# A sequence model on one core: another order of work where the local attention stage begins, and seven tiles in which a second queue issues part of the ring transfers

## The chip, the cores and the metric

The kernel runs on one core of a Trainium2 chip. The metric is the device time of one execution in microseconds (us). Before the change it is 1805.12 us, the median of three runs (1803.43 to 1805.38).

## What is computed

Four sequences of 1024 positions and 256 features go through two blocks. The first is causal attention with 16 heads of width 16. The second has two layers; each is a local attention with 8 heads of width 64 in windows of 128 positions, and a gated feed-forward part.

```python
def _layer(x, wqkv, qs, ksc, wo, lg, lb, w1, b1, w2, b2):
    h = shift_token(x)
    q, k, v = jnp.split(h @ wqkv, 3, axis=-1)
    q = l2norm(q) * qs
    k = l2norm(k) * ksc
    q, k = rotary_xpos(q, k)
    o = local_attention(q, k, v)      # own window and the one before it
    x = x + o @ wo
    h = layernorm(shift_token(x)) * lg + lb
    a, g = jnp.split(h @ w1 + b1, 2, axis=-1)
    return x + (a * gelu(g)) @ w2 + b2

x = x + attn(layernorm(x))
x = x + ffn(layernorm(x))             # two times _layer
```

All data is 32-bit floating point.

## The kernel before

**Stages.** The causal attention runs first, in 16 chunks (4 sequences by 4 groups of heads). Then comes the local stage: 64 tiles of 128 positions (2 layers, 4 sequences, 8 windows), taken in groups of four that alternate between two sequences. The feed-forward work of a finished group is spread over later tiles by a table of places (`F_PLAN`, and `F_FIRST` for the first group), which `feed(n, place)` reads.

**Queues.** The order of instructions on each engine is that of the program text: each engine works through its own queue in order, and an instruction that waits holds up all that stands behind it on its engine. TensorE (PE) does the matrix products, VectorE (DVE) and ScalarE (ACT) the work on what PE leaves in PSUM, GpSimd (POOL) powers, rotations and scalings in SBUF, and SyncE (SP) issues nearly all transfers.

**One tile of the local stage.** In iteration n of the loop at L1408 the core makes q, k and v of tile n (`qkv_mm`, L234; `qkv_take`: squares on ACT, L249, three products for each of q and k on DVE, L251 and L257, a copy of v on ACT, L265) and rotates them (`rotate`: a reduction on DVE, L273, and four operations on POOL, the power L279 and the product L281 among them). Scores of tile n - 2 are made (`scores`, L397 or L412), softened (`soften`: DVE L428, ACT L435) and scaled (`scale_e`, L449, on POOL or DVE). The weights of tile n - 4 meet v (`weigh`, L482 or L508), ACT copies the products out (`loT`, L490 or L515), and `attend` multiplies them by the output weights (`pw`, L524).

**The ring.** Before q, k and the softened weights can be operands, they have to be transposed into `ring`, a buffer of three slots. From tile 7 on `stage(n, e)` does it: DVE transposes blocks of 32 by 32 into `turned` (L308, L322, L323, or L331 for a tile without earlier keys), and 16 transfers (L339, from SP) carry the blocks to their partitions. Each waits until DVE has filled `turned`; DVE does not refill it until the transfers have read it. Scores and products of the next iterations wait until they have landed.

**The first tiles.** For the first tiles, and the last ones, PE does the transposing, since there is no time for transfers yet: `turn(n)` for q and k of tiles 0 to 6, with one copy of q on ACT and one of k on DVE (L353 and L354; both on ACT for tile 0), and `turn_e` for the weights of tiles 0 to 3 (L461, copies L466, DVE for even c and ACT for odd c). These tiles also run with shorter distances: scores of tile n - 1 and products of tile n - 2 for tiles 0 to 3. In iterations below 7 all scores of a tile come first (`scores(w, 0)`, `scores(w, 1)`), then the products with v, then the softening.

**The handover.** The end of the causal stage overlaps with the first tiles of the local stage: tile 1's q, k, v are made (L1356) while DVE transposes the last result (`put_oT`, L1155), whose transfers to `oT` are issued by SP and ACT (L1159). After `out_b` (L809, L1179) the rest of the plan runs (L1362): the normalising of a pair of rows (`out_c`, L706), statistics of another pair (`out_s`: L698, L699, a power on POOL, L163) and the normalising of that pair. Two more pairs have their statistics and normalising in iterations 2 to 4 of the local loop (L1469 to L1474), at the end of an iteration.

**PSUM.** All products of the local stage take turns in eight banks (`one`). A product into a bank waits until its former content has been read.

Of the kernel before, what the change touches and what calls it, by code (L numbers as in the profile page):

```python
# [17 lines left out]
B, T, D = 4, 1024, 256  # L18
NW = T // P
# [22 lines left out]
GRP = 4  # L42

SEGQ, SEGK, NSEG = 2 * LH, 2 * LH + 4, 2 * LH + 8
FAST_QK = 7
FAST = (4, 2)
EARLY = 2
# [4 lines left out]
def kernel_body(  # L52
# [17 lines left out]
    nc = tc.nc  # L70
# [7 lines left out]
    x_keep = keep.tile([B, P, NW, D], F32, name="x_keep")  # L78
# [93 lines left out]
    N = len(wins)  # L172
# [128 lines left out]
            state[n, "blocks"] = [(1 - behind, own), (int(behind), state[b, "kv"])]  # L301
        state[b, "kv"] = own

    def stage(n, e):

        k0, k1 = NSEG, 0
        if n is not None:
            nc.vector.transpose(  # L308
                turned[:, SEGQ:NSEG].rearrange("p k j r -> p (k j r)"),
                state.pop((n, "rot")).rearrange("p a d -> p (a d)"),  # L310
            )
            settle(n)
            k0, k1 = SEGQ, NSEG
        if e is not None:
            for g in range(2):
                dst = turned[:, LH * g : LH * g + LH]
                src = state.pop((e, "e", g))
                if slim(e):


                    dst = dst.rearrange("p (h b) j r -> p h (b j r)", b=2)
                    nc.vector.transpose(dst[:, :, 0:NK], src[:, :, 0:NK])  # L322
                    nc.vector.transpose(dst[:, :, NK : 2 * P], src[:, :, 0:HALF_W])  # L323
                    continue
                if wins[e][3] == 0:
                    dst = dst.rearrange("p (h b) j r -> p h b (j r)", b=2)[:, :, 1, :]
                    src = src[:, :, P : 2 * P]
                else:
                    dst = dst.rearrange("p k j r -> p (k j r)")
                    src = src.rearrange("p h k -> p (h k)")  # L330
                nc.vector.transpose(dst, src)  # L331
            k0, k1 = 0, max(k1, SEGQ)
        if k1 == 0:
            return
        i = (n + 1 if n is not None else e) % 3
        for d in range(4):
            for a in range(4):
                j = (a + d) % 4
                nc.sync.dma_start(  # L339
                    ring[32 * j : 32 * j + 32, i, k0:k1, 32 * a : 32 * a + 32],  # L340
                    turned[32 * a : 32 * a + 32, k0:k1, j, :],
                )

    def turn(n):

        rot = state.pop((n, "rot"))
        for a, k in ((0, SEGQ), (1, SEGK)):
            pt = one(f"pt{a}_{n}")
            for i in range(4):
                nc.tensor.transpose(  # L350
                    pt[:, i * P : (i + 1) * P], rot[:, a, i * P : (i + 1) * P], ident
                )
            copy = nc.vector.tensor_copy if a and n else nc.scalar.copy  # L353
            copy(ring[:, (n + 1) % 3, k : k + 4], pt.rearrange("p (c n) -> p c n", c=4))  # L354
        settle(n)

# [312 lines left out]
    def f_start(G):  # L669

        sooner = 6 if G == 0 else 3 if G == len(groups) - 1 else 0
        return 3 * (GRP * G + GRP + 3) + 2 - sooner
# [18 lines left out]
    stats, last_x = {}, []  # L691
# [19 lines left out]
    with actx:  # L711
# [73 lines left out]
        NCH = B * NC4  # L785
# [500 lines left out]
        n = -1  # L1286
# [26 lines left out]
        with tc.manual_schedule(  # L1313
            engines={
                mybir.EngineType.PE, mybir.EngineType.Activation, mybir.EngineType.DVE,
                mybir.EngineType.Pool, mybir.EngineType.SP,
            }
        ):

            warm = one("warm")  # L1320
            for _ in range(WARM):
                nc.tensor.matmul(warm[:, 0:P], lhsT=ident, rhs=ident, start=True, stop=True)
            nc.gpsimd.memset(qbuf[0], 0.0)
            nc.gpsimd.memset(kbuf[0], -1.0)
            nc.gpsimd.memset(nmax, 0.0)
            clear()
            norm(0, 0, NW // 2)
            for t2 in range(2):
                prep_x(0, t2)
                prep_a(0, t2)  # L1330
            for i in range(4):
                project(0, 0, i % 2, i // 2)
            spread(0, 0, nc.scalar)
            norm(0, NW // 2, NW)
            for t2 in range(2, 4):
                prep_x(0, t2)
                prep_a(0, t2)
            for i in range(4):
                project(0, 0, i % 2, 2 + i // 2)
            for n in range(-1, NCH):  # L1340
                if n == NCH - 1:
                    inner.close()
                    g1, g2, g3, g4, g5 = (
                        ctx.enter_context(tc.tile_pool(name=f"g{i}", bufs=i, side="right"))
                        for i in range(1, 6)
                    )
                for u in range(NU):
                    pair(n, u, 0)
                    pair(n, u, 1)
                    m, w = (n, u - 1) if u else (n - 1, NU - 1)  # L1350
                    if m >= 0:
                        products(m, w)
                    for fn, a in plan[n][u]:
                        fn(*a)
            products(NCH - 1, NU - 1)
            qkv_mm(1)  # L1356
            put_out(NCH - 1, 1)
            put_oT(NCH - 1, 1)
            qkv_take(1)
            rotate(1)  # L1360
            for t2 in (2, 3):
                out_b(B - 1, t2)  # L1362
            for fn, a in [x for u in plan[NCH] for x in u]:
                fn(*a)

# [25 lines left out]
    with tc.manual_schedule(  # L1393
# [12 lines left out]
            return [w for w in range(N) if w + (soon if fast(w) else late) == n]  # L1406

        for n in range(f_start(len(groups) - 1) // 3 + F_END // 3 + 2):  # L1408
            if EARLY <= n < N:
                qkv_mm(n, range(n == EARLY, 3))  # L1410
                qkv_take(n)
                if n == half - 1:
                    load_attn(1)
            r, m = (
                w if 0 <= w < N and not own(w) else None
                for w, own in ((n - 1, fast_qk), (n - 3, fast))
            )
            first = feed(n, 0, True)
            if first:
                feed(n, 0)  # L1420
            stage(r, m)
            if 0 < n <= N and fast_qk(n - 1):
                turn(n - 1)
                if n == EARLY - 1:
                    qkv_mm(EARLY, range(1))
            late = FAST_QK <= n < N - 1
            if EARLY <= n < N and not late:
                rotate(n)
            for w in at(n, 10 * N, 2):
                for c in range(4):  # L1430
                    turn_e(w, c)
            if EARLY <= n < N - 1:
                transposed(n + 1)
            if n in (half - 8, half):
                load_tab(1, n // half)
            if not first:
                feed(n, 0)
            now, then = at(n, 2, 1), at(n, 4, 2)

            end = n >= N - 1  # L1440
            now.sort(key=lambda w: not (end and fast(w)))
            begin = n < FAST_QK
            for step in (1, 0) if begin else (0, 1):
                for w in now if step else ():
                    for g in range(2):
                        scores(w, g)
                        if not begin:
                            soften(w, g)
                for w in () if step else then:
                    for c in range(4):  # L1450
                        weigh(w, c)
            for w in now:
                for g in range(2) if begin else ():
                    soften(w, g)
                keep_edge(w)
            if late:
                rotate(n)
            for w in then:
                attend(w)
                if w == half - 1:  # L1460
                    load_out(1)
            if n in (half - 7, half + 1):
                scale_tab(1, n // half)
            if not end:
                feed(n, 1)
            for w in now:
                scale_e(w, 0)
                scale_e(w, 1, nc.vector if begin or end and fast(w) else nc.gpsimd)
            for t2, first in ((2, EARLY), (3, EARLY + 1)):  # L1469
                src = last_x[0][:, 2 * t2 - GRP : 2 * t2 - GRP + 2, :] if last_x else None  # L1470
                if n == first:
                    out_stats(B - 1, t2, src, f2)
                if n == first + 1:
                    out_norm(B - 1, t2, src)  # L1474
            if n == EARLY + 2:
                nc.sync.dma_start(x_keep[B - 1][:, GRP:NW], last_x.pop())
            if end:
                feed(n, 1)
            feed(n, 2)
# [72 lines left out]
```

## Time and profile before

| | us |
|---|---|
| median of the runs | 1805.12 |
| the profiled execution, whole | 1806.02 |
| its span, first to last instruction | 1803.9 |
| TensorE busy | 1766.8 (98%) |
| VectorE busy | 1331.1 (74%) |
| ScalarE busy | 1019.5 (57%) |
| GpSimd busy | 1106.9 (61%) |
| ring transfers: issues of 96 KB and of 64 KB | 880 and 48 |

The busy shares are averages over stages. The causal stage takes about the first 600 us, the local stage the rest. A window line below gives, for a stretch of time, the busy time and number of instructions of each engine in it, the clock that was granted to TensorE as a share of full speed, the busy share of the core's 16 DMA engines, and GB/s. A waits line gives an engine and line, what it waited for, the sum in us, how many times, and the longest. A timeline line gives start, duration, engine, line, operation, what it writes and reads, and in brackets the idle time of the engine before it with what ended it. ACTq and SPq are the queues of ACT and SP at work on issuing a transfer.

### The profile page before, as it was taken

To read this page: it belongs to the slowest core of one execution; us is meant where nothing else is said; L and a number is where in the kernel's file an instruction comes from. 1 tells how busy PE (TensorE), PEld (TensorE's weight loads), DVE (VectorE), ACT (ScalarE), POOL (GpSimd) and SP (SyncE) were. 2 spreads that over 40 slices of the span, in tenths; PEclk is the share of its full clock that TensorE was granted. 3 is DMA by queue.
4 is the path that set the end of the run, shared out by engine and by line. 5 is a ranking of instruction groups with operands and counts; after the bars stand their busy time and mean duration, and the time that the engine had idled before them with its cause. 6 is when DMAs were issued, how large, how long until landed. Compare 5 with 4: busy or idle time off the path is not lost.

```text
span 1803.9 us, 45874 instructions
## 1 busy us (share of the span) xinstructions
PE 1766.8 (98%) x16922; PEld 1044.7 (58%) x16922; DVE 1331.1 (74%) x4107; ACT 1019.5 (57%) x2557; POOL 1106.9 (61%) x1310
## 2 busy tenths in 40 slices
PE   9999999999999898999999999999999999999999
PEld 5444454555444464565665656666656656566566
DVE  6987987887786677686776877767767768678642
ACT  1677767777777454545546455555555454545621
POOL 3354586476476566665766766757667667577511
PEclk8999999999999999999999999999999999999999
DMA  4435344335222202555556556655666555656420
GB/s 118 129 93 172 97 102 129 118 93 154 81 78 73 80 1 46 90 99 90 93 90 102 101 103 120 112 102 96 134 118 115 109 100 112 116 96 119 94 49 24
DMA packets 811294, 178.04 MB, mean 99 GB/s; under 512 B 761568, under 2 KB 786128, under 8 KB 810688
## 3 DMA queue, kind: packets, MB, share of 16 engines
q1 hardware_dynamic: 810752, 174.79, 45.6%
q8 instruction: 135, 2.21, 0.5%
q14 instruction: 87, 0.71, 0.1%
q10 hardware_dynamic: 320, 0.33, 0.1%
HBM read 50.32 MB, written 29.29 MB: 44 GB/s over the span
## 4 chain that ended last, share of the span: by engine, by line
PE 85%; DVE 7%; SPq 2%; DMA 2%; ACT 1%; issue 1%; POOL 1%; ACTq 0%; DVEq 0%; POOLq 0%
PE pag L614 16%; PE pf L638 9%; PE t L994 8%; PE av L1055 7%; PE pw L524 6%; PE s L994 6%; PE pq L234 5%; PE pv L234 5%; PE pk L234 5%; PE plo L482 5%; PE ls L397 4%; PE pp L809 3%; SPq L339 2%; PE pv L809 2%; DVE s L1004 1%
## 5 line engine op out<-in xcount | busy, mean ns | idle before, releaser
L1015 ACT ACTIVATE et<-t 128x512 f32<-128x512 f32 x558 | 292.2, 601 | 78.2 <-PE s L994 58.7
L614 PE MATMUL pag<-hnT,w 128*128 128x512 f32 x704 | 312.2, 593 | 0.8 <-DVE hnT L598 0.8
L994 PE MATMUL t<-qbuf,kbuf 32*128 32x512 f32 (+1 forms) x1488 | 297.9, 503 | 0.6 <-DMA qbuf<-way 0.3
L994 PE MATMUL s<-kbuf,qbuf 16*128 16x512 f32 (+3 forms) x1440 | 295.4, 506 | 1.5 <-DMA qbuf<-img 1.5
L435 ACT ACTIVATE e<-e,lnmx 128x192 f32<-128x192 f32 (+2 forms) x512 | 224.1, 439 | 50.2 <-DVE lnmx L428 49.7
L614 PEld LDWEIGHTS pag<-hnT,w 128*128 128x128 f32 x704 | 131.4, 190 | 142.5 <-issue 133.0
L449 POOL TENSOR_SCALAR e<-e,lrsum 128x192 f32<-128x192 f32 (+2 forms) x484 | 195.3, 426 | 18.1 <-DVE lrsum L446 12.6
L994 PEld LDWEIGHTS t<-qbuf,kbuf 32*128 32x128 f32 x1488 | 147.4, 184 | 92.0 <-ACT et L1015 40.4
L279 POOL TENSOR_TENSOR rn<-ss,mhalf 128x16 f32<-128x16 f32 x64 | 188.2, 2940 | 5.3
L1074 POOL TENSOR_TENSOR avs<-avs,part 128x512 f32<-128x512 f32 (+2 forms) x105 | 117.7, 1121 | 114.2 <-ACT part L1073 113.7
L276 POOL TENSOR_TENSOR rot<-rot,m 128x1024 f32<-128x1024 f32 x64 | 151.5, 2367 | 55.0 <-DVE m L257 45.4
L638 PE MATMUL pf<-w,act 128*128 128x256 f32 x768 | 173.1, 379 | 0.0
L994 PEld LDWEIGHTS s<-kbuf,qbuf 16*128 16x128 f32 x1440 | 144.9, 184 | 33.1 <-DVE nmax L1004 6.0
L638 PEld LDWEIGHTS pf<-w,act 128*128 128x128 f32 x768 | 145.8, 190 | 26.6 <-issue 7.2
L1004 DVE CUSTOM_DVE_ANT_0 s<-s,mask_c,mx 128x512 f32<-128x512 f32 (+1 forms) x240 | 132.8, 621 | 35.1 <-PE s L994 19.7
L1055 PE MATMUL av<-et,v_sb 128*32 128x512 f32 (+3 forms) x1536 | 155.2, 494 | 2.0 <-POOL et L1021 1.7
L628 DVE SCALAR_TENSOR_TENSOR act<-pag,cols_sb,ge 128x512 f32<-128x512 f32 x80 | 59.2, 740 | 132.4 <-ACT ge L627 94.8
L1021 POOL TENSOR_SCALAR_AFFINE_SELECT et<-et 128x256 f32<-128x256 f32 x256 | 98.9, 409 | 75.7 <-ACT et L1015 74.0
L1002 DVE TENSOR_REDUCE mx<-s 128x1 f32<-128x512 f32 (+1 forms) x240 | 133.4, 612 | 11.8 <-PE s L994 11.8
L278 POOL TENSOR_SCALAR ss<-ss 128x16 f32<-128x16 f32 x64 | 16.3, 255 | 195.7 <-DVE ss L273 191.0
L428 DVE CUSTOM_DVE_ANT_0 e<-ls,mask_h 128x192 f32<-128x192 f32 x408 | 116.7, 349 | 20.4 <-PE ls L397 20.4
L1004 DVE CUSTOM_DVE_ANT_0 s<-s,mask_c 128x384 f32<-128x384 f32 (+2 forms) x240 | 110.0, 522 | 28.5 <-PE s L994 28.4
(271 smaller groups left out, 3552.8 us busy)
## 6 DMA issues: line engine op xcount, KB each, us to landing
ring_sb<-turned SPq DMA_DIRECT2D x880, 96.0 KB
img<-dense SPq DMA_DIRECT2D x28, 256.0 KB
qbuf<-img SPq DMA_DIRECT2D x28, 256.0 KB
kbuf<-img SPq DMA_DIRECT2D x28, 256.0 KB
t<-recway SPq DMA_DIRECT2D x112, 64.0 KB
oway<-avs SPq DMA_DIRECT2D x28, 256.0 KB
xr<-x_keep SPq DMA_DIRECT2D x8, 512.0 KB
out_dram<-y_sb SPq DMA_DIRECT2D x16, 256.0 KB
```

What stands on the lines that cost most here:

```text
L234: nc.tensor.matmul(pq[i], lhsT=lhs[c], rhs=wt[:, c, i * INNER : (i + 1) * INNER], start=(c == 0), stop=(c == 1),)
L276: nc.gpsimd.tensor_tensor(rot, rot, m3, ALU.add)
L279: nc.gpsimd.tensor_tensor(rn[:, :, 0], ss, mhalf, ALU.pow)
L435: nc.scalar.activation(e[:, i, lo:nk], e[:, i, lo:nk], AF.Exp, bias=nmx[:, h : h + 1], scale=-1.0, accum_out=sums[:, h : h + 1],)
L449: by.tensor_scalar(e[:, i, lo:nk], e[:, i, lo:nk], rsum[:, h : h + 1], 1.0, ALU.mult, ALU.mult)
L614: nc.tensor.matmul(pg[half], lhsT=wt[:, c, ff * P : (ff + 1) * P], rhs=hnT[:, c, :], start=(c == 0), stop=(c == 1),)
L638: nc.tensor.matmul(pf[:, 0:D], lhsT=act[:, f, i * P : (i + 1) * P], rhs=wt[:, f, :], start=(f == 0), stop=(f == NF - 1),)
L994: nc.tensor.matmul(o, lhsT=lhsT, rhs=rhs, start=True, stop=True)
L1002: nc.vector.tensor_reduce(mxs[n + 1, i][:, h : h + 1], src, AX.X, ALU.max)
L1004: nc.vector.tensor_tensor_reduce(out=src, in0=src, in1=mask_c[:, 512 - w : 512], scale=1.0, scalar=mxs[n + 1, i][:, h : h + 1] if k0 else ...
L1015: nc.scalar.activation(et[:, h % 2, :], ts[h], AF.Exp, scale=ASCALE)
L1055: nc.tensor.matmul(av[32 * j : 32 * j + 32, c0:512], lhsT=v_sb[b % 2][:, kt, VW * (4 * c + j) : VW * (4 * c + j) + STRIP], rhs=ets[j // 2] ...
```

## The change

It has five parts:

- In iteration 7 the call of `stage` (tile 4's weights) moves from behind `qkv_mm` and `qkv_take` to ahead of them. In iterations 7 to 13 four of the 16 ring transfers (those with d = 3) are issued by ACT and not by SP.
- In `turn`, the copy of k of tiles 1 to 6 moves from DVE to ACT.
- At the handover, all of the remaining plan but its last entry moves ahead of `qkv_take(1)`, `rotate(1)` and `out_b`; the last entry, a normalising with its store, stays behind them.
- In iterations below 7, the products with v move from behind both halves of the scores to between them.
- Statistics and normalising of the two late pairs of rows, and their store, move from the end of an iteration to ahead of `attend`.

```diff
@@ -301,7 +301,7 @@
             state[n, "blocks"] = [(1 - behind, own), (int(behind), state[b, "kv"])]
         state[b, "kv"] = own
 
-    def stage(n, e):
+    def stage(n, e, shared=False):
 
         k0, k1 = NSEG, 0
         if n is not None:
@@ -336,7 +336,7 @@
         for d in range(4):
             for a in range(4):
                 j = (a + d) % 4
-                nc.sync.dma_start(
+                (nc.scalar if shared and d == 3 else nc.sync).dma_start(
                     ring[32 * j : 32 * j + 32, i, k0:k1, 32 * a : 32 * a + 32],
                     turned[32 * a : 32 * a + 32, k0:k1, j, :],
                 )
@@ -350,7 +350,7 @@
                 nc.tensor.transpose(
                     pt[:, i * P : (i + 1) * P], rot[:, a, i * P : (i + 1) * P], ident
                 )
-            copy = nc.vector.tensor_copy if a and n else nc.scalar.copy
+            copy = nc.vector.tensor_copy if a and n >= FAST_QK else nc.scalar.copy
             copy(ring[:, (n + 1) % 3, k : k + 4], pt.rearrange("p (c n) -> p c n", c=4))
         settle(n)
 
@@ -1356,12 +1356,14 @@
             qkv_mm(1)
             put_out(NCH - 1, 1)
             put_oT(NCH - 1, 1)
+            *left, (fn, a) = [x for u in plan[NCH] for x in u]
+            for f, z in left:
+                f(*z)
             qkv_take(1)
             rotate(1)
             for t2 in (2, 3):
                 out_b(B - 1, t2)
-            for fn, a in [x for u in plan[NCH] for x in u]:
-                fn(*a)
+            fn(*a)
 
 
 
@@ -1406,19 +1408,22 @@
             return [w for w in range(N) if w + (soon if fast(w) else late) == n]
 
         for n in range(f_start(len(groups) - 1) // 3 + F_END // 3 + 2):
+            r, m = (
+                w if 0 <= w < N and not own(w) else None
+                for w, own in ((n - 1, fast_qk), (n - 3, fast))
+            )
+            if n == FAST_QK:
+                stage(r, m, True)
             if EARLY <= n < N:
                 qkv_mm(n, range(n == EARLY, 3))
                 qkv_take(n)
                 if n == half - 1:
                     load_attn(1)
-            r, m = (
-                w if 0 <= w < N and not own(w) else None
-                for w, own in ((n - 1, fast_qk), (n - 3, fast))
-            )
             first = feed(n, 0, True)
             if first:
                 feed(n, 0)
-            stage(r, m)
+            if n != FAST_QK:
+                stage(r, m, FAST_QK < n < 2 * FAST_QK)
             if 0 < n <= N and fast_qk(n - 1):
                 turn(n - 1)
                 if n == EARLY - 1:
@@ -1440,21 +1445,30 @@
             end = n >= N - 1
             now.sort(key=lambda w: not (end and fast(w)))
             begin = n < FAST_QK
-            for step in (1, 0) if begin else (0, 1):
-                for w in now if step else ():
-                    for g in range(2):
-                        scores(w, g)
-                        if not begin:
-                            soften(w, g)
-                for w in () if step else then:
-                    for c in range(4):
-                        weigh(w, c)
+            for w in now if begin else ():
+                scores(w, 0)
+            for w in then:
+                for c in range(4):
+                    weigh(w, c)
+            for w in now:
+                for g in range(begin, 2):
+                    scores(w, g)
+                    if not begin:
+                        soften(w, g)
             for w in now:
                 for g in range(2) if begin else ():
                     soften(w, g)
                 keep_edge(w)
             if late:
                 rotate(n)
+            for t2, first in ((2, EARLY), (3, EARLY + 1)):
+                src = last_x[0][:, 2 * t2 - GRP : 2 * t2 - GRP + 2, :] if last_x else None
+                if n == first:
+                    out_stats(B - 1, t2, src, f2)
+                if n == first + 1:
+                    out_norm(B - 1, t2, src)
+            if n == EARLY + 2:
+                nc.sync.dma_start(x_keep[B - 1][:, GRP:NW], last_x.pop())
             for w in then:
                 attend(w)
                 if w == half - 1:
@@ -1466,14 +1480,6 @@
             for w in now:
                 scale_e(w, 0)
                 scale_e(w, 1, nc.vector if begin or end and fast(w) else nc.gpsimd)
-            for t2, first in ((2, EARLY), (3, EARLY + 1)):
-                src = last_x[0][:, 2 * t2 - GRP : 2 * t2 - GRP + 2, :] if last_x else None
-                if n == first:
-                    out_stats(B - 1, t2, src, f2)
-                if n == first + 1:
-                    out_norm(B - 1, t2, src)
-            if n == EARLY + 2:
-                nc.sync.dma_start(x_keep[B - 1][:, GRP:NW], last_x.pop())
             if end:
                 feed(n, 1)
             feed(n, 2)
```

## The prediction

> **What bounds the kernel.** I read the waits of TensorE first, then busy time by stretches, then the timeline from 600 to 830 us, the only stretch that the change touches (tiles 1 to 14 of the 64 of the local stage). TensorE (PE) is the bound. The columns below are busy time of PE, weight load, DVE, ACT and POOL, then the clock granted to PE, then the DMA share.
>
> ```profile
> 600.00:620.00 20.00, 19.14 (x150) 10.07 (x142) 12.46 (x36) 3.55 (x9) 10.16 (x9) 1.00 0.10 34
> ...
> 620.00:640.00 20.00, 15.95 (x65) 9.84 (x66) 13.09 (x55) 11.69 (x44) 10.71 (x12) 0.74 0.41 138
> ...
> 760.00:780.00 20.00, 15.07 (x174) 10.52 (x173) 10.99 (x33) 7.15 (x27) 13.93 (x21) 0.99 0.62 107
> ...
> 780.00:785.00 5.00, 4.63 (x113) 4.55 (x117) 4.64 (x11) 0.65 (x2) 0.00 (x0) 0.50 0.20 48
> ...
> 820.00:840.00 20.00, 20.00 (x134) 10.61 (x130) 12.98 (x36) 10.52 (x27) 10.70 (x12) 0.98 0.49 83
> ...
> 1200.00:1700.00 500.00, 499.96 (x4586) 316.00 (x4585) 371.73 (x1105) 267.77 (x760) 345.50 (x370) 1.00 0.60 111
> ```
>
> From 820 us on PE is full; a later search of its waits from 820 to 1760 us gives 3.1 us in all. So whatever PE gains or loses before 820 us reaches the end one for one. In 600 to 820 us it is busy 197.3 of 220 us (the eleven rows of 20 us added), 22.7 us idle, and after some idle stretches the clock is halved. The waits, with us in total, times, longest:
>
> ```profile
> PE plo L482 <- DMA ring_sb<-turned: 8.1, 6, 1.9
> ...
> PE plo L508 <- DMA ring_sb<-turned: 3.4, 1, 3.4
> ...
> PE plo L508 <- DVE ring_sb L466: 3.2, 2, 2.1
> ...
> PE pw L524 <- ACT loT L515: 2.7, 4, 0.7
> ...
> PE ls L412 <- DVE ring_sb L354: 2.2, 2, 1.6
> ...
> PE pn L592 <- DVE m L257: 1.7, 1, 1.7
> ...
> PE pe L461 <- POOL e L449: 1.4, 1, 1.4
> ```
>
> Those on L482 and the 3.4 us on L508 are ring transfers that land late (tiles 8, 11, 12, 14); the others belong to tiles 2 to 8.
>
> **The handover and tiles 1 to 6.** These are the parts on L1356 to 1366, L353 and L1443 to 1476.
>
> ```profile
> 603.55 1.88 PE L234 MATMUL pk<-wqkv,hT 128*128 128x512 f32 x4
> ...
> 604.68 1.41 ACTq L1159 DMA_DIRECT2D oT<-t  x2
> ...
> 606.14 0.60 ACT L249 ACTIVATE m<-pq 128x512 f32<-128x512 f32 x1 [6.57 <-PE pk L234]
> ...
> 618.72 0.73 DVE L706 TENSOR_SCALAR y_sb<-x,mvo,rs_o 128x256 f32<-128x256 f32 x2 [5.08 <-POOL rs_o L163]
> ```
>
> First: in the last row DVE sits 5.08 us, from 613.64, on one reciprocal root that POOL makes late. Behind it in DVE's queue stands the softmax of tile 0, whose scores were ready at 615.88. The change issues the statistics before the second qkv is taken: 0.73 us of normalising and 1.37 us of statistics (DVE rows 611.62 to 613.64), in a gap in which DVE idled 2.12 us (604.65 to 606.77), and POOL, which makes the root, idles until 609.46; so they cost nothing, and 2.1 us there if that gap were gone. The softmax starts near 616.0 and not at 619.37, 3.4 us sooner. Exponentials (3.1 us) then end near 619.5, and PE's turns of tile 0's weights end near 621.3 where they ended at 625.1.
>
> Second, the copy of the keys (L354) goes to ACT. DVE made it after its six rotations (626.50); ACT has it after two squares and the v copy (1.75) and two ring copies (1.2), near 622.4, and tile 1's first scores start there and not at 627.23. ACT's own price is 0.59 us a tile, in tiles where it is busy about 10 of 20 us.
>
> Third, the products go between the score halves. For tile 0 they must wait for DVE's copy of the turned weights: scaling until 620.6, rotations (2.6) until 623.2, reduction 1.2, copy 0.4, so 624.8. Products end near 626.1, scores at 627.1, and the output product (pw), which started at 633.60, starts at 627.1: 6.5 us gained. About 2 us of that is the clock, 0.50 from 625 to 630, where 2.0 us of scores took 3.78.
>
> For tiles 3 and 4 the copy of the products (0.59) hides behind the second scores' half (1 us): 0.69 + 0.69 us of waits go. The waits of 0.60 (scores of tile 3) and 1.14 us (products of tile 3) on DVE go because DVE loses a copy of 0.68 and its statistics move into its wait for pw. The store of L1476 only goes ahead on SP, which issues nothing else in tile 4: nothing. Sum 6.5 + 1.4 + 1.7 = 9.6, say **10 us gained**. Bounds: 5 (the products wait for DVE as long as PE did) and 12.
>
> **The shared transfers, tiles 7 to 13.** Each tile issues 16 transfers; SP takes 0.66 us for each, and the last lands 2.2 us after its issue. With 12 on SP the ring is full some 2.6 us sooner, enough for the late landings (1.2 + 1.2, 1.8 + 1.2, 1.9 + 0.9 us). What is queued behind the four on ACT? Here is tile 10:
>
> ```profile
> 746.68 0.59 ACT L265 COPY vt<-pv 128x512 f32<-128x512 f32 x1 [1.12 <-PE pv L234]
> ...
> 750.07 0.40 DVE L323 STREAM_TRANSPOSE turned<-e 128x256 f32<-128x256 f32 x1
> ...
> 750.28 19.86 SPq L339 DMA_DIRECT2D ring_sb<-turned  x20
> ...
> 750.32 0.65 ACT L490 COPY loT<-plo 128x256 f32<-128x256 f32 x2 [1.02 <-PE plo L482]
> ...
> 751.56 1.99 PE L524 MATMUL pw<-wlo,loT 128*128 128x256 f32 x8
> ```
>
> ACT's queue goes in order. The handover rows show that an issue blocks it: pq was there at 603.6, but its square ran at 606.14, just after two issues of 1.41 us together that had waited for DVE until 604.65. The releaser named there, pk, had ended at 605.4. So an ACT transfer costs 0.70 us (1.41/2; the eight at 14.78 and 20.77 us took 2.60 and 2.93 for four), and before it ACT waits until DVE has filled `turned`. In tile 10 that is 750.47, while ACT was free at 747.27. Behind the four (2.8 us) stand hT with its edges (0.65), the gelu (0.65), the copies of the products (0.65) and the exponentials. PE's pw of tile 6 waits for those copies: 750.47 + 2.8 + 0.65 + 0.65 + 0.65 = 755.2, where it began at 751.56. **3.6 us lost in tile 10**, in place of a wait for DMA in another tile.
>
> The same for the others, counted from the start of each tile's qkv to pw. Tile 7: its stage now stands ahead of the qkv of tile 7 in ACT's queue too. DVE is busy with the first FFN's norm until 696.5, its two transposes of 0.65 end at 697.8, four issues at 700.6, then squares and v copy (1.75), two ring copies (1.2), hT (0.5): the qkv of tile 8 can start at 704.0, not at 699.42, so 4.6 lost. Tile 8: DVE's rotation of tile 7 is late by the same block (701.2), then 2.5 of it, softmax 2.2, reduction 1.2, POOL's power and product 5.3, scaling 3.25, transpose 1.2, four issues 2.8, hT 0.65, a table load 1.28, gelu 0.62, copy 0.6: pw at 722.8 against 715.42, 7.4 in all, so 2.8 more; the 3.4 us wait on L508 is swallowed in it. Tile 9: `turned` full 9.1 us in, and 2.8 + 0.65 + 0.65 + 0.65 more is 13.9 against 11.95: 1.9. Tile 11: exponentials end 3.4 us in, POOL's power and scaling at 10.3, transpose 11.6, + 4.1 (no gelu) = 15.8 against 13.7: 2.1. Tile 12: 13.0 against 14.1, a gain of 1.1. Tile 13: `turned` full 9.6 us in, pw 13.7 against 8.5: 5.2. Tile 14 has no shared issue left, and its landing of 2.8 us and the slow clock behind it (1.6) go: 4.4 gained. Sum 4.6 + 2.8 + 1.9 + 3.6 + 2.1 − 1.1 + 5.2 − 4.4 = **14.7 us lost**. Bounds: a ring transfer that ACT issues is nowhere in this trace. At SP's shortest issue (0.585) the seven stages are about 5 us cheaper; at 1.0 us (towards the longest of SP, 1.8) 9 dearer.
>
> **The clock.** Six of the new stalls are 3.6 to 7 us long. Of the old ones, 1.8 + 1.2 us at 777 us was followed by 0.50 (products, scores and pw of tile 12 took 8.0 for 5.2 us of work), 1.9 + 0.9 at 813 by 1.6 us more, 3.4 us at 709 by nothing (1.00). So each costs 0 to 2.8; I take 1.5, **9 us lost**, bounds 0 and 17.
>
> **Sum:** −10 + 14.7 + 9 = +13.7. The profiled execution took 1806.0 us around its span of 1803.9, the median is 1805.1; on the median that is **1819 us**.
>
> **Two rules weighed.** The Trainium skill, "DMA: Bandwidth & Descriptors", section "Issuing engines are not separate DMA queues", says that starting transfers from several engines saves only the starter's time, usually small, since all run on the same 16 engines. It speaks against this part; the rows go part of the way with it: the 16 are busy 0.81 to 0.92 of the time while a stage runs freely (743 to 746 us), so at most a fifth of some 10 us, 2 us, is to be had. By the rule alone the landings would not move, the sum would lose tile 14's gain of 4.4 and be +18. The same skill, "TensorE: Matmul & The Clock Gate", Part 1, has PE fall to half rate after about 3.4 us of idleness and recover after as long; the row at 777 us fell after less, the one at 709 us not at all. By the page, six falls would cost 6 × 1.7 = 10 us, an estimate.
>
> **Rivals.**
> (a) *ACT has room, and the waits go.* ACT is busy 7 to 13 of 20 us. If work behind the issues is not missed, −10 stands, with the DMA waits (11.5) and the slow clock after them (4.4): −26, 1779. If half of the block shows, it is midway to the forecast's +13.7: −6, 1799. For it: TensorE's largest waits are these. Against it: the square at 606.14, and loT, which pw needs at once, behind `turned` in every one of the tiles.
> (b) *The clock does not fall.* −10 + 14.7 = +4.7, 1810, or 1805 with issues at SP's shortest. For it: the 3.4 us stall at full clock.
> (c) *Two issuers crowd the 16 engines.* Issue on ACT stretches to 1.0 us, +9, with clock 12: 1831; at 1.2 us 1837. Decided where four ACT issues last over 3.5 us. For it: 0.92 DMA share with SP alone.
>
> **How the numbers follow.** Forecast (1811 to 1829): 0.52. (a) 0.26, (b) 0.12, (c) 0.10. The range runs from 1796, into (a), to 1838, which leaves out 0.13 below (most of (a)'s lower half) and 0.05 above; the likeliest's own range is 1808 to 1831. About 0.2% (3.6 us) is what a measurement can tell from none: faster 0.24 (nearly all of (a)); same 0.08 (half of (b), the top of (a)); slower 0.68 (the forecast, (c), the other half of (b)).
>
> **What would show it.** Right: ACT issues in seven tiles at some 0.7 us, each beginning when `turned` is full; hT and loT after them; waits "pw on loT" of 2 to 6 us in tiles 8 to 13; the waits for ring transfers nearly gone; the first scores of tile 1 near 622; clock below 1 between 690 and 820 us more often. Wrong: pw of tile 10 still about 10 us after its qkv begins; ACT squares running before issues that stand ahead of them. Then (a) holds.

## The result, and the profile after

| | us |
|---|---|
| before, median of 4 runs on the same chip | 1804.97 |
| after, median of 4 runs (1824.14 to 1828.27) | 1825.72 |
| ratio after to before, 95% interval | 1.0118 [1.0103, 1.0133] |
| the profiled execution after, whole, and its span | 1825.63, 1823.4 |

The change made the kernel 20.75 us slower. The forecast was 1819 us with a range of 1796 to 1838: the side is right and so is the place; the time is 6.7 us above the forecast, and the loss 7.0 us above the sum's +13.7.

First the waits of TensorE after the change (total us, times, longest), to be held against the list in the prediction:

```profile
PE pw L524 <- ACT loT L490: 20.1, 5, 5.2
PE ls L397 <- ACT vt L265: 6.8, 1, 6.8
PE pw L524 <- ACT loT L515: 6.3, 2, 5.6
PE plo L508 <- DVE ring_sb L466: 3.7, 2, 2.1
...
PE plo L482 <- DMA ring_sb<-turned: 0.4, 1, 0.4
```

The waits for ring transfers, 8.1 + 3.4 us before, are down to 0.4 us: that part of the change did what it was meant to do. In their place stand 33.2 us of waits in which ACT is named, on the copies of the products (loT) and once on the copy of v. (0.7 of the 6.3 us on L515 is a wait ahead of tile 7 that was there before; 1.4 us on hT, in tile 9, is in none of the rows shown.)

Now busy time by stretches of 20 us, in the columns of the prediction's first fence (after the change the same tiles lie up to 22 us later):

```profile
600.00:620.00 20.00, 19.18 (x153) 10.36 (x144) 14.54 (x51) 7.40 (x27) 11.57 (x12) 1.00 0.42 139
620.00:640.00 20.00, 18.30 (x138) 13.19 (x137) 17.93 (x56) 12.07 (x38) 15.08 (x12) 1.00 0.09 34
...
760.00:780.00 20.00, 14.80 (x160) 9.79 (x160) 11.98 (x35) 7.07 (x28) 12.52 (x14) 0.84 0.40 65
780.00:800.00 20.00, 15.32 (x163) 10.67 (x162) 11.81 (x45) 6.10 (x24) 8.68 (x13) 0.84 0.50 86
...
840.00:860.00 20.00, 20.00 (x173) 10.69 (x172) 11.70 (x31) 10.53 (x29) 10.70 (x12) 1.00 0.48 81
```

Two opposite changes show. From 620 to 640 us TensorE gained 2.4 us of work and its clock rose from 0.74 to 1.00: the handover is better. From 680 to 840 us it is full nowhere, and the clock in the stretch of tiles 7 to 14 (676 to 850 us) is 0.89 in the mean, where it was 0.96. The same columns for that stretch, before and then after:

```profile
676.00:850.00 174.00, 159.35 (x1448) 97.97 (x1445) 120.84 (x369) 86.98 (x262) 113.88 (x119) 0.96 0.47 81
```

```profile
676.00:850.00 174.00, 139.45 (x1233) 86.26 (x1230) 102.33 (x324) 74.15 (x229) 100.83 (x111) 0.89 0.44 72
```

The DMA engines are busy 0.44 of those 174 us, where it was 0.47: they are not what holds the core. From 840 us on TensorE's waits are alike: from there to the end both kernels have the same rows, but for the 0.4 us above. The span grew by 19.5 us, and tile 15's qkv starts 17.6 later. Of the 1.9 us behind that, 1.6 arise in one place near the end, behind a wait that both kernels have; the last section shows it.

The timeline of TensorE shows the handover. These are tile 1's first scores, tile 0's products, and tile 0's output product, which the prediction put at 622.4, 624.8 and 627.1 us:

```profile
621.62 1.14 PE L412 MATMUL ls<-ring_sb 64*128 64x256 f32 x8
...
624.34 1.09 PE L508 MATMUL plo<-ring_sb,vt 128*64 128x128 f32 x16 [1.58 <-DVE ring_sb L466]
...
626.43 1.99 PE L524 MATMUL pw<-wlo,loT 128*128 128x256 f32 x8
```

Each came within 0.8 us of it. Next, tile 10 after the change, ScalarE's timeline, to be held against the prediction's fence of the same tile, where loT began 3.6 us after the copy of v:

```profile
747.72 0.59 ACT L265 COPY vt<-pv 128x512 f32<-128x512 f32 x1 [1.12 <-PE pv L234]
751.93 3.83 ACTq L339 DMA_DIRECT2D ring_sb<-turned  x4
755.80 0.37 ACT L211 COPY hT<-py 128x256 f32<-128x256 f32 x1 [7.49 <-DMA ring_sb<-turned]
...
756.42 0.69 ACT L622 ACTIVATE ge<-pag,cols_sb 64x512 f32<-64x512 f32 x1
757.13 0.65 ACT L490 COPY loT<-plo 128x256 f32<-128x256 f32 x2
```

DVE's timeline, the last of the transposes that fill `turned` for that stage:

```profile
751.50 0.40 DVE L323 STREAM_TRANSPOSE turned<-e 128x256 f32<-128x256 f32 x1
```

The 7.49 us in brackets are two things one after the other: from 748.3 to 751.9 us ACT starts nothing, since the first issue at the head of its queue waits for that transpose; from 751.93 to 755.76 it issues. hT, the gelu and loT, whose products TensorE had made by 747.9, 749.6 and 751.3 us, come after. "Idle" on ACT is here the time in which the queue is held, and the releaser in brackets is the transfer's issue, not a landing.

What that does to TensorE, tiles 8 to 14, the output product of each (and, behind tile 10's, the qkv that follows):

```profile
712.43 3.78 PE L524 MATMUL pw<-wlo,loT 128*128 128x256 f32 x8 [5.64 <-ACT loT L515]
...
737.11 1.99 PE L524 MATMUL pw<-wlo,loT 128*128 128x256 f32 x8 [0.45 <-ACT loT L490]
...
757.83 3.78 PE L524 MATMUL pw<-wlo,loT 128*128 128x256 f32 x8 [5.16 <-ACT loT L490]
761.40 3.15 PE L234 MATMUL pq<-wqkv,hT 128*128 128x512 f32 x4
...
779.04 3.78 PE L524 MATMUL pw<-wlo,loT 128*128 128x256 f32 x8 [5.20 <-ACT loT L490]
...
799.37 3.78 PE L524 MATMUL pw<-wlo,loT 128*128 128x256 f32 x8 [4.68 <-ACT loT L490]
...
822.34 3.49 PE L524 MATMUL pw<-wlo,loT 128*128 128x256 f32 x8 [4.64 <-ACT loT L490]
...
838.48 1.99 PE L524 MATMUL pw<-wlo,loT 128*128 128x256 f32 x8
```

Each late loT costs twice: the wait itself, 4.6 to 5.6 us, and then eight products that take 3.49 to 3.78 us where they took 1.99. Tile 14, the first without a shared issue, is clean at once.

### The profile page after: what moved, and what is told of

Read it like the earlier page. It is cut to its first block, busy times and chain, and to the rows that moved or that the text cites. A ratio compares the mean times of both kernels' runs of the same rounds, so it can differ in the third digit from the quotient of the medians.

```text
span 1823.4 us, 45886 instructions
## 1 busy us (share of the span) xinstructions
PE 1770.9 (97%) x16922; PEld 1047.3 (57%) x16922; DVE 1330.3 (73%) x4101; ACT 1022.6 (56%) x2563; POOL 1107.6 (61%) x1310
## 4 chain that ended last, share of the span: by engine, by line
PE 84%; DVE 8%; POOL 2%; ACT 2%; issue 1%; DMA 1%; ACTq 1%; SPq 1%; DVEq 0%; POOLq 0%
PE pag L614 15%; PE pf L638 9%; PE t L994 8%; PE pw L524 7%; PE av L1055 7%; PE s L994 6%; PE pq L234 5%; PE pk L234 5%; PE pv L234 5%; PE plo L482 4%; PE ls L397 3%; PE pp L809 3%; PE pv L809 2%; PE plo L508 1%; PE pr L809 1%
## 5 line engine op out<-in xcount | busy, mean ns | idle before, releaser
L524 PE MATMUL pw<-wlo,loT 128*128 128x256 f32 x512 | 135.7, 411 | 26.4 <-ACT loT L490 20.1
```

The costliest lines, as they stand in the source:

```text
L524: nc.tensor.matmul(pw[:, 0:D], lhsT=oT[:, c, :], rhs=wt[:, c, :], start=(c == 0), stop=(c == 3))
```

## The experiments

Ratios are to runs of the kernel before on the same chip; "us" is (ratio − 1) times 1805. The intervals are some 0.001 to 0.002 to each side, 2 to 3.5 us, and a difference between two kernels carries both.

| kernel | median | before | ratio | us |
|---|---|---|---|---|
| after | 1825.72 | 1804.97 | 1.0118 [1.0103, 1.0133] | +21.3 |
| e1_sp_only | 1789.62 | 1804.04 | 0.9926 [0.9914, 0.9939] | −13.4 |
| e2_share_only | 1838.18 | 1804.04 | 1.0186 [1.0170, 1.0202] | +33.6 |
| e3_after_products | 1786.74 | 1804.04 | 0.9902 [0.9887, 0.9918] | −17.7 |
| e4_one_of_16 | 1802.37 | 1804.04 | 0.9991 [0.9981, 1.0002] | −1.6 |
| e5_wait_alone | 1801.35 | 1806.29 | 0.9974 [0.9965, 0.9983] | −4.7 |
| e7_no_early | 1796.60 | 1806.29 | 0.9953 [0.9939, 0.9967] | −8.5 |
| p1_out | 1802.34 | 1806.29 | 0.9980 [0.9969, 0.9990] | −3.6 |
| p4_out_copy | 1799.21 | 1806.29 | 0.9961 [0.9949, 0.9974] | −7.0 |
| c1_fill | 1820.50 | 1806.72 | 1.0084 [1.0066, 1.0103] | +15.2 |
| e6_every_tile | 1789.40 | 1806.72 | 0.9907 [0.9890, 0.9924] | −16.8 |
| e8_seven_on_sp | 1788.74 | 1806.72 | 0.9907 [0.9889, 0.9926] | −16.8 |

**e1_sp_only: the changed kernel with all 16 transfers on SP again.**

```diff
-                (nc.scalar if shared and d == 3 else nc.sync).dma_start(
+                nc.sync.dma_start(
```

> The changed kernel with all 16 transfers of a stage back on SP; all else of the change stays, the early stage of tile 7 too. Theory (ScalarE's queue is held up by the four issues, which stand ahead of work that TensorE waits for): what is left is the handover's gain, some 10 us, and the old waits for late transfers in tiles 11, 12 and 14 return: 1795 us, 1791 to 1798, faster than before. Rival (the early stage of tile 7, or the handover's new order, costs the time): 1805 or more.

It ran at 1789.62 us: 34.7 us faster than the changed kernel by the ratios, and 13.4 us faster than before, just below the expected 1791 to 1798. TensorE's waits in it:

```profile
PE plo L482 <- DMA ring_sb<-turned: 5.7, 6, 1.3
...
PE pq L234 <- DVE m L257: 2.0, 1, 2.0
```

The ACT waits are gone and the ring transfers are late again, six times, by 1.3 us at the most. The whole loss, and more than it, is in who issues four of 16 transfers.

**e2_share_only: the kernel before with the shared issue and tile 7's early stage alone.**

```diff
...
-                nc.sync.dma_start(
+                (nc.scalar if shared and d == 3 else nc.sync).dma_start(
...
+            if n == FAST_QK:
+                stage(r, m, True)
...
-            stage(r, m)
+            if n != FAST_QK:
+                stage(r, m, FAST_QK < n < 2 * FAST_QK)
```

> The kernel before with only the shared issue of tiles 7 to 13 and the early stage of tile 7. Theory (the parts add up): 1826 + 10 = 1836 us, 1832 to 1840. Rival (the faster first tiles make the later stalls worse, as TensorE arrives earlier): about as the changed kernel, 1822 to 1829.

1838.18 us: the two halves of the change add. Their difference, 33.6 − 21.3 = 12.3 us, is what the handover parts give beside the shared issue; alone (e7) they give 8.5. The two agree within their intervals, 4.0 and 2.5 us to each side.

**e3_after_products: the same four transfers on ACT, but behind the copies loT in its queue.**

```diff
-                (nc.scalar if shared and d == 3 else nc.sync).dma_start(
+                move = (
...
+                if shared and d == 3:
+                    state.setdefault("later", []).append(move)
+                else:
+                    nc.sync.dma_start(*move)
...
                     weigh(w, c)
+            for move in state.pop("later", ()):
+                nc.scalar.dma_start(*move)
```

> The changed kernel, with the same four transfers on ScalarE in the same tiles, but issued in its queue behind hT, gelu and the copies of the products (loT), ahead of the exponentials. Theory (the place in ScalarE's queue costs the time, not the transfers): TensorE's waits on loT go and the late landings shrink: 1792 us, 1788 to 1798. Rival (two issuers crowd the 16 DMA engines, or ScalarE's time for issuing is what costs): the transfers and their issue time are the same, so 1815 or more.

1786.74 us, just below the expected 1788 to 1798, faster than both kernels, and 39 us faster than the changed one with the same transfers from the same engine. ScalarE's timeline in tile 10 (the new lines shift line numbers by four; L1458 is the issue):

```profile
740.03 0.65 ACT L494 COPY loT<-plo 128x256 f32<-128x256 f32 x2 [1.02 <-PE plo L486]
741.88 2.82 ACTq L1458 DMA_DIRECT2D ring_sb<-turned  x4
744.79 1.28 ACT L439 ACT_TABLE_LOAD   x1 [4.11 <-DVE lnmx L432]
```

The issues still wait for `turned` (until 741.85 us here) and still take 2.82 us, but only the exponentials stand behind them, which begin some 2 us later than DVE's first `lnmx`, the row maximum that they need (742.4 + 0.3 us). Every pw of tiles 7 to 14 took 1.99 us and waited for no loT. What is left of late transfers:

```profile
PE plo L486 <- DMA ring_sb<-turned: 2.2, 2, 1.2
```

So the price was neither the transfers nor most of ACT's time, but the place in its queue.

A small part of ACT's time still shows. In tile 13 the exponentials start 2.7 us behind DVE's first `lnmx` (789.0 us), held by the issues; DVE's reciprocal waits for them, an operand of the feed-forward part (hnT) stands behind that reciprocal in DVE's queue, and in tile 14 TensorE waits 2.19 us for it. ACT, DVE and TensorE:

```profile
791.70 0.45 ACT L439 ACTIVATE e<-e,lnmx 128x192 f32<-128x192 f32 x1 [6.45 <-DVE lnmx L432]
...
795.34 0.18 DVE L450 RECIPROCAL lrsum<-lsum 128x4 f32<-128x4 f32 x1 [1.57 <-ACT e L439]
...
796.27 3.70 PE L618 MATMUL pag<-hnT,w 128*128 128x512 f32 x8 [2.19 <-DVE hnT L602]
```

In e1 the same product waits for nothing.

**e4_one_of_16 and e5_wait_alone: what of the price is the wait for `turned`, and what the issues?** The first leaves one transfer on ACT in the changed kernel's place. The second leaves none; ACT copies one column of the filled `turned`, a copy that nothing reads, in the same place, and so has the wait without an issue.

```diff
-                (nc.scalar if shared and d == 3 else nc.sync).dma_start(
+                (nc.scalar if shared and d == 3 and a == 3 else nc.sync).dma_start(
```

```diff
...
+        if shared:
+            seen = g4.tile([P, 1], F32, tag="seen", name=f"seen_{n}_{e}")
+            nc.scalar.copy(seen, turned[:, SEGQ - 1, 3, 31:32])
...
-                (nc.scalar if shared and d == 3 else nc.sync).dma_start(
+                nc.sync.dma_start(
```

> The changed kernel with one transfer of 16 on ScalarE, not four. Theory: ScalarE still waits until VectorE has filled the staging buffer, and saves three issues of 0.7 to 0.95 us a tile; TensorE's waits on loT fall by some 2 to 3 us each: 1810 us, 1806 to 1815. Rival (the cost is in proportion to the transfers that ScalarE issues): a quarter of the way from the kernel with all on SP to the changed one, 1803 if the former is 1795.

> The changed kernel with all 16 transfers on SP, and in the seven tiles, where ScalarE's issues stood, a copy of one column on ScalarE that reads the staging buffer and so waits until VectorE has filled it. Theory (two costs: the wait for the staging buffer, and the issues themselves): one issue a tile cost 12.8 us over the kernel with all on SP, four 36, so 7.8 for each issue and 5 for the wait: 1795 us, 1792 to 1800. Rival (only the issuing counts): as with all on SP, 1788 to 1791.

Measured 1802.37 and 1801.35 us. Against e1 the wait alone costs 0.0048 × 1805 = 8.7 us, more than expected (e5 lies above its 1792 to 1800); the first issue 0.0017, 3.1 us; the other three 0.0127, 22.9 us; each of the three to within some 3 us. So e4 came out below the expected 1806 to 1815, a third of the way from e1 to the changed kernel. That is nearer to the rival of costs in proportion to the number, which says a quarter, though a fixed part is there, of 8.7 us. Three rows of e5, ScalarE's timeline, tiles 9 to 11, with the idle time that ends when `turned` is full:

```profile
726.74 0.19 ACT L338 COPY seen<-turned 128x1 f32<-128x1 f32 x1 [3.24 <-DVE turned L323]
...
743.95 0.19 ACT L338 COPY seen<-turned 128x1 f32<-128x1 f32 x1 [3.24 <-DVE turned L323]
...
760.97 0.19 ACT L338 COPY seen<-turned 128x1 f32<-128x1 f32 x1 [7.14 <-DVE turned L323]
```

And e4's pw in tiles 10 to 12, TensorE's timeline:

```profile
745.81 2.00 PE L524 MATMUL pw<-wlo,loT 128*128 128x256 f32 x8 [1.55 <-ACT loT L490]
...
761.48 3.56 PE L524 MATMUL pw<-wlo,loT 128*128 128x256 f32 x8 [2.58 <-ACT loT L490]
...
778.47 3.59 PE L524 MATMUL pw<-wlo,loT 128*128 128x256 f32 x8 [2.43 <-ACT loT L490]
```

One issue already makes waits of 2.4 to 2.8 us in tiles 8 and 11 to 13, and these already slow pw to 3.5 us; in tile 7 the wait for the copy of v is 4.8 us, and 4.1 in e5.

**c1_fill: what of the price is the clock?** The changed kernel, with five products of 128x512 that nothing reads between scores and pw in iterations 8 and 10 to 13, so that TensorE is busy while it waits.

```diff
+            if n in (8, 10, 11, 12, 13):
+                idle = one(f"idle_{n}")
+                for _ in range(5):
+                    nc.tensor.matmul(
+                        idle, lhsT=ident, rhs=layer[0]["wqkv"][:, 0, 0:INNER], start=True, stop=True
+                    )
             if late:
```

> The changed kernel with five added products of 128x512 (some 4.3 us, their result is read by nothing) in TensorE's queue between the scores and pw of tiles 8, 10, 11, 12 and 13, where it stalls 4.6 to 5.6 us. Theory (a stall of that length halves the granted clock, which makes pw 3.5 to 3.8 us for 2.0 and what follows 0.1 to 1.3 longer, 12 us in the five tiles): pw takes 2.0 again, 1814 us, 1811 to 1818. Rival (the slow pw is not due to the idle time, or is hidden behind ScalarE's work anyway): 1823 or more.

1820.5 us, between the theories and 6.1 us below the changed kernel, to within 4.3 us, so the total does not settle the size. The clock from 676 to 850 us rose from 0.89 to 0.97, and every pw took 1.89 to 1.99 us. But the fill has a price of its own, as TensorE's timeline shows for tiles 10 and 11:

```profile
754.11 6.26 PE L1465 MATMUL idle<-wqkv,ident 128*128 128x512 f32 x10 [3.74 <-ACT hT L211]
760.20 1.89 PE L524 MATMUL pw<-wlo,loT 128*128 128x256 f32 x8
...
773.03 4.56 PE L1465 MATMUL idle<-wqkv,ident 128*128 128x512 f32 x10
778.12 1.99 PE L524 MATMUL pw<-wlo,loT 128*128 128x256 f32 x8 [0.53 <-ACT loT L490]
```

In tile 11 it fits. In tiles 8 and 10 it needs a PSUM bank that hT, itself behind the issues, has to empty, starts 3.23 and 3.74 us late, and in tile 10 runs long at a low clock, ahead of pw. By tile it is clearer. From one tile's qkv to the next, tile 10 is 2.8 us longer than in the changed kernel; tile 11, with the pq at its head, is 4.1 us shorter and tile 12 2.7, against 4.0 and 2.8 us by which the changed kernel's rows there (pq, pw and pf) are longer than at full clock. So where the fill fits, it takes away what the slow rows cost; what the clock costs in all seven tiles this run does not show.

**The other parts: e7_no_early (e1 with tile 7's stage back behind its qkv), p1_out (the kernel before with the plan's rest moved ahead, and no more), p4_out_copy (that, and the copy of k on ACT).**

```diff
-            if n == FAST_QK:
-                stage(r, m, True)
...
-            if n != FAST_QK:
-                stage(r, m, FAST_QK < n < 2 * FAST_QK)
+            stage(r, m)
```

> All transfers on SP, and the stage of tile 7 back behind its qkv; the handover's new order stays. Theory (the early stage is worth something by itself: it puts TensorE's wait of 2.0 us for VectorE in place of 3.4 us for late transfers, and gives the next stages an earlier start): 1793 us, 1791 to 1796. Rival (it only moves a wait): 1788 to 1791, as with it.

> The kernel before with only the plan's rest moved ahead at the handover. Theory (the softmax of tile 0 starts 3.4 us sooner, but the scores of tile 1 still wait for VectorE's copy of the keys): 1801 us, 1798 to 1802.5. Rival (worth nothing without the other parts): 1804 within 1.

> The kernel before with the plan's rest moved ahead and the copy of the keys on ScalarE; scores and products in the old order, statistics at the old place. Theory (these two hold most of the handover's 10 us): 1797 us, 1795 to 1799. Rival (the order of scores and products holds most of it): 1801 or more.

By the differences: statistics ahead 3.6 us, the copy of k 3.4 more, products between the halves and the late statistics 1.5, tile 7's early stage on SP 4.9; each of the last three to within some 3 us, so the 1.5 cannot be told from nothing. The first two kernels came within 2.2 us of what was expected. e7 did not: beside e1's 1789.6 it had been put at 1793, 3.4 us for the early stage, and the ratios give 4.9, with an interval of 1.5 to 8.3 us that holds both.

**Can e3 be bettered?** e6_every_tile issues so in every tile from 7 on (`n > FAST_QK`), e8_seven_on_sp leaves tile 7's stage wholly to SP (`stage(r, m)`).

> Four transfers on ScalarE behind the copies of the products, now in every tile from 7 on. Theory (after tile 14 TensorE has no waits that an earlier landing could shorten): as with seven tiles, 1787 us within 3. Rival (ScalarE's 2.8 us a tile reach TensorE in later tiles, which have more feed-forward work on ScalarE): 1795 or more.

> As the run with the four transfers behind the copies of the products, but tile 7's early stage wholly on SP. Theory (tile 7's transfers have time to spare; ScalarE's first table load and exponentials come sooner): the same or up to 2 us less, 1784 to 1788. Rival (tile 8 waits for late transfers again): 1789 or more.

0.9907 both, where e3 had 0.9902: no difference that can be told, and e8's 1788.74 is just above its 1784 to 1788. TensorE's wait for hnT in tile 14 is 2.4 us in e8 and 0.4 in e6. All three are below e1's 0.9926, but e3's gain over e1, 4.3 us, is hardly larger than the uncertainty of the difference, some 3.6 us. Issuing from a second engine is worth little even where it costs little.

## Why the prediction came out as it did

**Handover and tiles 1 to 6, −10: right.** The qkv of tile 7 starts at 676.22 us where it started at 686.33: 10.1 us. Run by itself (e7) the part is worth 8.5, to within 2.5. The chain behind it held step by step in the fence above. Its parts were shared out as the experiments say, not as the sum had them: the products between the halves, on which 6.5 us were hung together with the earlier softmax and copy, bring, with the late statistics, no more than 1.5 once these two are there.

**Shared transfers, tiles 7 to 13, +14.7, and clock, +9: right mechanism, clock too small.** From one tile's qkv to the next, after minus before:

| tile | predicted, without clock | measured, with clock |
|---|---|---|
| 7 | +4.6 | +5.6 |
| 8 | +2.8 | +3.3 |
| 9 | +1.9 | +2.2 |
| 10 | +3.6 | +7.0 |
| 11 | +2.1 | +6.6 |
| 12 | −1.1 | +1.4 |
| 13 | +5.2 | +6.2 |
| 14 | −4.4 | −4.6 |
| sum | +14.7 (+9 = +23.7) | +27.7 |

The seven blocks stand where they were put, tile 12's as a loss, and tile 14 gains what was said. Over the forecast with its clock the surplus is 4.0 us, most of it in tiles 10 and 11. The term that was mis-sized is "So each costs 0 to 2.8; I take 1.5". Adding up how much longer the rows behind the six long stalls took than at full clock (pq is the product for q, pn and pf are work of the feed-forward part; pw 4 × 1.79 + 1.50; behind tile 10's the pq, 1.27; behind those of tiles 11 and 12 the pf, 0.90 and 0.98; 0.1 behind tile 8's; in tile 7 the scores, pn and pq, 2.5) gives 14.4 us, 2.4 a stall and not 1.5. Without them 27.7 − 14.4 = 13.3 us are left, against 14.7 (both hold the old kernel's slow rows as a gain); tile 10 is then 5.2 us longer, its four issues having taken 3.83 us and not 2.8, and tile 12 1.3 us shorter, as forecast. That 14.4 is a sum of rows, not a measured difference; c1 confirms it for tiles 11 and 12. The 1.9 us behind tile 15 are in no term of the sum.

**The price of an issue, 0.70 us: nearly right.** Four took 2.73, 3.06, 3.16, 3.83, 3.14, 2.85 and 2.83 us in tiles 7 to 13, 0.77 each in the mean. Tile 10's 3.83 passes the point of 3.5 us that rival (c) was to be decided by; the mean, 3.09, does not. Over the sum's price that is 0.07 us an issue, 2 us over the seven tiles; no run shows how much of it is crowding. It is not what costs: in e3 four took 2.74 to 3.72 us. The lower bound was worked out wrongly: at 0.585 us an issue, 28 issues are 3.2 us cheaper, not 5, and rival (b)'s 1805 would be 1807.

**Tile 7: right size, another way.** The prediction had tile 8's qkv wait for hT. What waits first is a bank, for a half of its scores, behind the copy of v (ACT's queue, ACT, then TensorE):

```profile
686.79 2.73 ACTq L339 DMA_DIRECT2D ring_sb<-turned  x4
689.57 0.60 ACT L249 ACTIVATE m<-pq 128x512 f32<-128x512 f32 x1 [7.93 <-DMA ring_sb<-turned]
```

```profile
691.18 2.04 PE L397 MATMUL ls<-ring_sb 64*64 64x64 f32 x32 [6.84 <-ACT vt L265]
```

**The rivals.** (a), that ACT has room, is refuted where the issues stand and nearly true some 2 us of work further back: e3 is (a) with hT, the gelu and loT let past, at 1787 us. (b), that the clock stays, is refuted by every pw of 3.5 us and more. **Not foreseen:** that the shared issue would undo a kernel 13 us faster than before; the sum held the pieces (−10, and the early stage in the tile terms) but priced the early stage only with its issues on ACT.

## What to carry to other kernels

In an engine that works its queue in order, the price of a transfer handed to it is the time until its source is full, plus all issues, for everything behind it; ask what stands next in that queue and who waits for that, and put the issues behind it. Here the same four issues cost 34.7 us ahead of hT, the gelu and loT, and less than they gave behind them. Where the bound engine is made to stall for some us, add the slower work behind the stall: here, by the rows, 2.4 us on top of each 4.6 to 6.8.

## What the runs showed of the hardware

The clock did not follow the length of a stall in any simple way. Waits of 1.86 to 2.84 us (e4, e5) were followed by pw of 2.5 to 3.6 us, one of 1.55 us by 2.00, and the same wait of 3.4 us in tile 8 had scores and pw of 1.57 and 1.99 us behind it in the kernel before (TensorE's timeline):

```profile
712.90 1.09 PE L508 MATMUL plo<-ring_sb,vt 128*64 128x128 f32 x16 [3.36 <-DMA ring_sb<-turned]
...
715.42 1.99 PE L524 MATMUL pw<-wlo,loT 128*128 128x256 f32 x8
```

and these in p1_out:

```profile
708.29 1.09 PE L508 MATMUL plo<-ring_sb,vt 128*64 128x128 f32 x16 [3.38 <-DMA ring_sb<-turned]
709.32 2.50 PE L397 MATMUL ls<-ring_sb 64*64 64x64 f32 x64
711.75 2.67 PE L524 MATMUL pw<-wlo,loT 128*128 128x256 f32 x8
```

Near the end of the kernel both wait 2.08 us at the same place, and the 32 products behind it take 1.97 us before the change and 3.52 after. These are 1.6 us of the 1.9 that the span lost behind tile 15's qkv. Before, then after:

```profile
1712.07 1.97 PE L508 MATMUL plo<-ring_sb,vt 128*64 128x128 f32 x32 [2.08 <-DVE ring_sb L466]
```

```profile
1730.11 3.52 PE L508 MATMUL plo<-ring_sb,vt 128*64 128x128 f32 x32 [2.08 <-DVE ring_sb L466]
```

The Trainium skill, "TensorE: Matmul & The Clock Gate", Part 1, puts the fall after about 3.4 us of idleness and describes a window that runs freely, so that the phase counts. The two pairs above agree with a free phase; the falls after 1.9 to 2.8 us are earlier than the figure.

Shared issuing made SP's own issues longer. In tiles 7 to 13, 16 issues on SP took 10.8 to 12.0 us before, 0.71 each in the mean; 12 on SP with four on ACT took 8.3 to 10.3 us, 0.79 each, and one on ACT up to 0.96 in a tile's mean. What four on ACT took off SP's time was therefore about 1.8 us a stage, 9.5 against 11.3 in the mean, and not a quarter of 11.3, which is 2.8. The runs do not show why.
